# Outer combinations of x made in the round that takes them, and GpSimd's combinations in pieces of 512 columns

## The chip, the cores and the metric

The kernel runs on one core of one Trainium2 chip. The metric is the device time in microseconds of one execution; the time given is the median of several runs. A profiled execution is one run of its own: its span is the stretch that the hardware profiler covers, and its time is a little longer than the span. All data are 32-bit floats.

## The reference

Two layers, each a residual around "a convolution conditioned on a small vector, then a feed-forward". Layer 1 mixes the 128 channels with a matrix of its own per batch entry and then applies a 2048x2048 weight to the positions, with a low-rank update; layer 2 is a grouped convolution of 9 taps and a feed-forward of 16 heads on permuted rows:

```python
agg_w = einsum('bk,koi->boi', att, weight)          # layer 1: att from cond
y = einsum('boi,bih->boh', agg_w, x) + agg_b
out = einsum('bsd,od->bso', y, W) + bias + upd      # upd: low rank, from A and Bf
x = x + out
...
x = x + unpermute(down(gelu(up(permute(conv(x) + ctx)))))   # layer 2
```

x is 32 x 128 x 2048. The change touches only the product of x with the 2048x2048 weight.

## The kernel before, in words

**The product.** The kernel folds the low-rank update into the weight (16 blocks of 128x2048, in DRAM as `wb_d`) and multiplies x with it by a fast scheme of 7 products in place of 8 (Strassen's, in Winograd's form), used twice, one inside the other. The outer level gives seven **rounds**, in the order P1, P2, P6, P7, P5, P3, P4 (L48). Each round has eight **steps**, one for each group g of four batch entries; step i is round i // 8, group i % 8. The inner level gives, within a step, seven products of four 128x512 matmuls each (`multiply`, L318), which TensorE does in the order P1, P2, P6, P5, P7, P3, P4. The profile counts two matmul records for each matmul, so a step has 56.

**Left sides.** x lies in DRAM transposed, in four tiles per group: `x_load(g, tp, kh)` (L251) fetches one of 1 MB (128x2048). The outer scheme needs, per group, x00, x01, x11 as they are; s1 = x10 + x11; s2 = s1 - x00; x00 - x10 (P7); x01 - s2 (P3). Before, `x_loads` of round P1 fetches x00, x10 and x11 together, `x_combine` puts them on the list `outer`, and `x_outer` (L298) makes s1 and s2 right there on GpSimd, two operations over 2048 columns (L302, L304), and stores each in DRAM (`part_store`, on GpSimd's queue). Round P6 loads s2, round P5 loads s1, round P3 loads x01 and s2. `x_combine` (L275) makes the outer difference where its round has one (L280 for P7, L282 for P3: one operation over 2048 columns) and then the four inner combinations into a tile `s_...` (L285 to L288, 512 columns each), all on GpSimd.

**Right sides.** `outer_weights` (L365) loads up to three weight blocks for one kc of the next round; its `combine` (L385), called a step later, makes one block of them on GpSimd over 2048 columns (L387, L389; for P6 the result is stored as t2). `inner_weights` (L232) makes from the four blocks the inner combinations on GpSimd, 512 columns each: for each block t1 (L239), t2 (L240), then b22 - b12 **written over b12** (L241), then t4 (L242). Product P6 of a step takes t2, P5 takes t1, P7 the overwritten one, P4 takes t4. For round P1 the four blocks are made first (`w_make`, L162), each is stored to DRAM from GpSimd's queue (L160), and `make_first` interleaves the making with `inner_weights`; after block 2 comes the inner combination of the first group's x. For round P2 it runs in the step of group 6, later in that of group 7.

**Results.** A step of P1 copies its sums from the PSUM banks into a fresh tile `m_P1...` (first copies on ScalarE, L329; additions on VectorE, L327); a step of a later round loads old sums from DRAM (`part_load`) and adds to them. A store on SP's queue ends each step (L363). A bank taken by a product comes free for a later one only when VectorE or ScalarE has read it.

**Order.** The order on each engine is the program's: nothing is reordered. In a step i after round P1 stand: GpSimd's `x_combine` for step i + 1; SP's loads of x for step i + 2; SP's load of old sums for i + 1; in group 7 `inner_weights` for the next round; the outer-weight combinations of the step before; in groups 2 to 5 SP's loads of outer weights; the seven products. In round P1, x is loaded one step ahead, and the steps make the other twelve weight blocks (`w_make_two`, L205, additions L213) ahead of their products, from combinations of A (`a_combine`, GpSimd) and of Bf (`b_combine`, L193; for the first of them VectorE, L196 to L199, queued behind the additions that make the first four blocks). Between the products (`between`), VectorE also makes `mixed_kernel` (L407, L409: 128x128 operations into `ags`, a pair after each of four products, in groups 0 to 5 of the rounds after P1) and, in P1, sums of weight rows (L230, L951, L952).

**Slots.** All large tiles share 24 slots of 128x2048 in SBUF. A tile takes the slot that was released longest ago, and its first writer waits until the last reader of the tile before it is done, a store included.

After round P4 comes the second layer's feed-forward (L679, L690), which the change does not touch.

Of the kernel before, what the change touches and what calls it, by code (L numbers as in the profile page):

```python
# [51 lines left out]
def adaln_ffn_kernel(  # L52
# [35 lines left out]
    def scratch(name, shape=(P, L)):  # L88
# [12 lines left out]
    ag_d = [scratch(f"ag_d{i}") for i in range(B // NCH)]  # L101
    part_d = {
        (n, g): scratch(f"{n}_d{g}")
        for n in ("s1", "s2", "p1", "u1", "u2", "u3", "c00", "c01", "c10", "c11")
        for g in range(NG)
    }

# [124 lines left out]
    def inner_weights(name, ts, between=lambda kc: None):  # L232

        t1, t2, t4 = (slot(f"{name}_t{k}", (P, 4, QW)) for k in (1, 2, 4))
        tt = nc.gpsimd.tensor_tensor
        for kc, t in enumerate(ts):
            between(kc)
            b11, b12, b21, b22 = (t[:, ki, oi] for ki in range(2) for oi in range(2))
            tt(t1[:, kc], b12, b11, ALU.subtract)  # L239
            tt(t2[:, kc], b22, t1[:, kc], ALU.subtract)  # L240
            tt(b12, b22, b12, ALU.subtract)  # L241
            tt(t4[:, kc], b21, t2[:, kc], ALU.subtract)  # L242
        return {
            "P1": [t[:, 0, 0] for t in ts], "P2": [t[:, 1, 0] for t in ts],
            "P3": [t[:, 1, 1] for t in ts], "P7": [t[:, 0, 1] for t in ts],
            "P4": [t4[:, kc] for kc in range(4)], "P5": [t1[:, kc] for kc in range(4)],
            "P6": [t2[:, kc] for kc in range(4)],
        }


    def x_load(g, tp, kh):  # L251
        t = slot(f"xt_{g}{tp}{kh}", (P, 2, 2, QW))
        nc.sync.dma_start(t.rearrange("p k s c -> p (k s c)"), xT[g, tp, kh])
        return t
# [6 lines left out]
    def part_store(n, g, t, eng=nc.gpsimd):  # L261
        eng.dma_start(part_d[n, g], t.rearrange("p k s c -> p (k s c)"))

    def x_loads(r, g):
        return {
            "P1": lambda: [x_load(g, 0, 0), x_load(g, 1, 0), x_load(g, 1, 1)],
            "P2": lambda: [x_load(g, 0, 1)],
            "P6": lambda: [part_load("s2", g)],
            "P7": lambda: [x_load(g, 0, 0), x_load(g, 1, 0)],
            "P5": lambda: [part_load("s1", g)],  # L270
            "P4": lambda: [x_load(g, 1, 1)],
            "P3": lambda: [x_load(g, 0, 1), part_load("s2", g)],
        }[r]()

    def x_combine(r, g, ts):  # L275

        a = ts[0]
        tt = nc.gpsimd.tensor_tensor
        if r == "P7":
            tt(a, a, ts[1], ALU.subtract)  # L280
        if r == "P3":
            tt(a, a, ts[1], ALU.subtract)  # L282
        s = slot(f"s_{r}{g}", (P, 4, QW))
        a11, a12, a21, a22 = a[:, 0, 0], a[:, 1, 0], a[:, 0, 1], a[:, 1, 1]
        tt(s[:, 0], a21, a22, ALU.add)  # L285
        tt(s[:, 1], s[:, 0], a11, ALU.subtract)
        tt(s[:, 2], a11, a21, ALU.subtract)
        tt(s[:, 3], a12, s[:, 1], ALU.subtract)  # L288
        if r == "P1":
            outer.append((g, ts))  # L290
        return {
            "P1": a11, "P2": a12, "P3": s[:, 3], "P4": a22,
            "P5": s[:, 0], "P6": s[:, 1], "P7": s[:, 2],
        }

    outer = []

    def x_outer():  # L298
        tt = nc.gpsimd.tensor_tensor
        while outer:  # L300
            g, (a, b, c) = outer.pop(0)
            tt(b, b, c, ALU.add)  # L302
            part_store("s1", g, b)
            tt(c, b, a, ALU.subtract)  # L304
            part_store("s2", g, c)


    ADDED = {
# [56 lines left out]
    def outer_weights(r, kc):  # L365

        def get(d):
            t = slot(f"wo_{r}{kc}", (P, 2, 2, QW))
            nc.sync.dma_start(t.rearrange("p k o c -> p (k o c)"), d)
            return t  # L370

        def w(kh, oh):
            return wb_d[kh, oh, kc]

        tt = nc.gpsimd.tensor_tensor
        srcs = {
            "P6": [w(1, 1), w(0, 1), w(0, 0)],
            "P7": [w(1, 1), w(0, 1)],
            "P5": [w(0, 1), w(0, 0)],
            "P4": [w(1, 0), t2_d[kc]],  # L380
            "P3": [w(1, 1)],
        }[r]
        ts = [get(d) for d in srcs]

        def combine():  # L385
            if len(ts) > 1:
                tt(ts[0], ts[0], ts[1], ALU.subtract)  # L387
            if len(ts) > 2:
                tt(ts[0], ts[0], ts[2], ALU.add)  # L389
                nc.gpsimd.dma_start(t2_d[kc], ts[0].rearrange("p k o c -> p (k o c)"))  # L390
            return ts[0]

        return combine
# [465 lines left out]
        b_load(1, q)  # L859
    for k in blocks[4:6]:  # L860
        wt[k] = w_load(*k)
    xs[0] += [x_load(0, 1, 0), x_load(0, 1, 1)]
    nc.gpsimd.memset(wsum, 0.0)
    lhs, sa, tb = {}, {}, {}
    sa[0] = a_combine(0, nc.gpsimd.tensor_tensor)
# [23 lines left out]
    for i, (r, g) in enumerate(steps):  # L889
        ri = i // NG  # L890
        last_round = ri + 1 == len(ROUNDS)
        if i + 1 < len(steps):
            if i + 1 not in xs:
                xs[i + 1] = x_loads(*steps[i + 1])
            if not last_round:
                lhs[i + 1] = x_combine(*steps[i + 1], xs.pop(i + 1))
                x_outer()
        if i + 2 < len(steps) and ri > 0 and not last_round:
            xs[i + 2] = x_loads(*steps[i + 2])
        if i == 0:  # L900
            olds_load(0)
        if i + 1 < len(steps) and not last_round:
            olds_load(i + 1)
        if g == NG - (1 if ri else 2) and ri < len(ROUNDS) - 1:
            nxt = inner_weights(ROUNDS[ri + 1], [nxt[kc] for kc in range(4)])

        if ri == 0:
            ks = blocks[4 + 2 * g : 6 + 2 * g]
            if ks:
                two = [wt.pop(k) for k in ks]  # L910
                w_make_two(ks, two, sa[ks[0][0]], tb[ks[0][1]])
                made.extend(ks)
                if g == 1:
                    a_scale(1, 0, 4)
                    sa[1] = a_combine(1, nc.gpsimd.tensor_tensor)
                if g == 3:
                    tb[0] = b_combine(0, nc.gpsimd.tensor_tensor)
                for k, t in zip(ks, two):
                    unsummed.append((k[1], t))
                    if k[:2] == (1, 0):  # L920
                        nxt[k[2]] = t
        elif ri + 1 < len(ROUNDS):
            for k, combine in waiting.items():
                nxt[k] = combine()
            waiting = {}
            if 2 <= g < 6:
                waiting[g - 2] = outer_weights(ROUNDS[ri + 1], g - 2)

        if last_round and g == 0:
            late_loads()  # L930
        if last_round and g == 2:

            late["te"] = mix.rearrange("p (k r) c -> p k r c", k=2)
            nc.sync.dma_start(mix.rearrange("p k c -> p (k c)"), te_d)
        k0 = 3 * (g - NG)
        if last_round:
            stage(k0, stage_first)

        def between(j):
            b = (ri - 1) * (NG - 2) + g  # L940
            if ri > 0 and g < NG - 2 and b < B and j < KEXP // 2:
                mixed_kernel(b, (2 * j, 2 * j + 1))
            if ri == 0 and j == 2:
                for k in blocks[6 + 2 * g : 8 + 2 * g]:
                    wt[k] = w_load(*k)
            if ri == 0 and j in (1, 3) and unsummed:
                row_sums(*unsummed.pop())
            if ri == 0 and j == 5 and unsummed_first:
                t = unsummed_first.pop(0)
                tt = nc.vector.tensor_tensor  # L950
                tt(wsum[:, 0, 0], wsum[:, 0, 0], t[:, 0, 0], ALU.add)  # L951
                tt(wsum[:, 0], wsum[:, 0], t[:, 1], ALU.add)  # L952
            if last_round:
                if j == 3 and i + 1 < len(steps):
                    lhs[i + 1] = x_combine(*steps[i + 1], xs.pop(i + 1))
                    olds_load(i + 1)
                if j in (2, 4):
                    stage(k0 + j // 2, stage_first)
                if j % 2:
                    stage_third(k0 + j // 2)  # L960
                else:
                    stage(k0 + j // 2, stage_second)

        multiply(r, g, lhs.pop(i), rhs, olds.pop(i), between)
        next(chain, None)
        if last_round and g >= 6:
            pair(g - 6)
        if last_round and g == 7:
            rings()
            gather_two(0)  # L970
        if g == NG - 1 and ri + 1 < len(ROUNDS):
            rhs = nxt
            nxt = {}
# [84 lines left out]
```

## Time and profile before

| What | us |
|---|---|
| Time, median of 3 runs (2677.62 to 2681.15) | 2679.33 |
| The profiled execution, its own time | 2674.35 |
| Its span | 2672.6 |
| TensorE busy, 6484 matmul records | 2623.7 |
| VectorE busy | 1385.7 |
| GpSimd busy | 1142.4 |
| ScalarE busy | 535.1 |
| Start of round P1's first product | 48.6 |
| Start of round P2 / P6 / P7 / P5 / P3 | 333.9 / 526.3 / 718.5 / 913.9 / 1106.2 |
| Start of the feed-forward | 1547 |

A stretch line of the profile gives the bounds of a stretch, its length, the busy time of each engine with the number of instructions, the granted clock of TensorE (1.00 is full speed), the share of the DMA engines and the rate. A line of waits reads "engine, what waited, what ended the wait: total, times, longest". A line of the chain of waits gives start, length and what ran. A line of the timeline gives start, length, engine, line, operation, out<-in, shapes and, in brackets, the idle time before it and what ended it.

### The profile page before, as it was taken

Reading aid. Unit: us, or ns where it says so; the run is one execution under the profiler, and the core shown is the slowest. Engines: PE = TensorE matmul, PEld = TensorE weight load, DVE = VectorE, ACT = ScalarE, POOL = GpSimd, SP = SyncE. Lnnn points to the kernel's source line nnn. Section 1 sums busy time; section 2 is a strip of 40 time slices with the busy share of each in tenths; the row PEclk is TensorE's granted clock in tenths of the full one; section 3 lists DMA queues with packets and bytes.
Section 4 is the critical chain, followed back from the end, with each engine's and each line's share of the span. In section 5 each row is a group of like instructions: output and inputs, shape, how many; then the busy total and the mean of one; then the engine's idle time right before and its main releaser. Section 6 shows DMA issues by size and latency. Waiting matters only on the chain.

```text
span 2672.6 us, 19881 instructions
## 1 busy us (share of the span) xinstructions
PE 2623.7 (98%) x6484; PEld 1234.4 (46%) x6484; DVE 1385.7 (52%) x2168; ACT 535.1 (20%) x1103; POOL 1142.4 (43%) x770
## 2 busy tenths in 40 slices
PE   7899999999999999999999999999999999999998
PEld 3344444444444444444444455545455554555543
DVE  3666145233255355454256666666666666666610
ACT  0000100000000000000001144444444444444432
POOL 6655636624646521755323223434333343333222
PEclk9899999999999999999999999999999999999999
DMA  7786557535456466556575788777787777877532
GB/s 314 276 319 253 217 204 306 200 144 223 189 206 262 161 265 249 219 226 236 194 258 174 246 296 282 234 229 234 243 251 226 228 227 233 249 234 235 164 127 87
DMA packets 183607, 609.16 MB, mean 228 GB/s; under 512 B 16848, under 2 KB 88016, under 8 KB 139088
## 3 DMA queue, kind: packets, MB, share of 16 engines
q1 hardware_dynamic: 148928, 466.40, 49.5%
q0 software_dynamic: 34144, 140.53, 15.3%
q8 instruction: 52, 0.85, 0.1%
q10 hardware_dynamic: 432, 0.96, 0.1%
q14 instruction: 51, 0.42, 0.0%
HBM read 364.03 MB, written 210.24 MB: 215 GB/s over the span
## 4 chain that ended last, share of the span: by engine, by line
PE 92%; DVE 4%; POOL 2%; issue 1%; DMA 1%; SPq 0%; ACT 0%; POOLq 0%; DVEq 0%; ACTq 0%
PE bank L334 47%; PE bank L679 16%; PE bank L690 16%; PE bank L537 6%; PE bank L447 4%; PE bank L210 2%; DVE ags L409 2%; DVE u L327 0%; DVE vb L516 0%; DMA ws<-in_ffw 0%; DVE vb L519 0%; DVE va L517 0%; DMA a_sb<-in_A 0%; DVE va L518 0%; POOL wsum L874 0%
## 5 line engine op out<-in xcount | busy, mean ns | idle before, releaser
L679 PE MATMUL bank<-t,ws 128*128 128x512 f32 x1024 | 460.4, 592 | 0.2 <-DMA ws<-in_ffw 0.2
L690 PE MATMUL bank<-gl,ws 128*128 128x512 f32 x1024 | 460.2, 592 | 0.0
L334 PE MATMUL bank<-P_t,s_P 128*128 128x512 f32 x896 | 395.6, 595 | 22.3 <-ACT m_P L329 22.3
L697 POOL DMA_INDIRECT out<-t,orow x128 | 152.6, 1192 | 568.7 <-DVE t L695 496.2
L682 ACT ACTIVATE gl<-bank 128x512 f32<-128x512 f32 x512 | 306.2, 598 | 445.9 <-PE bank L679 443.5
L327 DVE TENSOR_TENSOR u<-bank,u 128x512 f32<-128x512 f32 x280 | 187.3, 687 | 389.6 <-PE bank L334 380.5
L690 PEld LDWEIGHTS bank<-gl,ws 128*128 128x128 f32 x1024 | 194.8, 190 | 232.7 <-issue 230.8
L679 PEld LDWEIGHTS bank<-t,ws 128*128 128x128 f32 x1024 | 194.7, 190 | 226.8 <-issue 219.3
L334 PE MATMUL bank<-wo_P,s_P 128*128 128x512 f32 x640 | 285.5, 596 | 5.2 <-DVE u L327 5.2
L334 PEld LDWEIGHTS bank<-P_t,s_P 128*128 128x128 f32 x896 | 171.1, 191 | 236.9 <-issue 213.0
L438 ACT ACTIVATE bank<-w,aggb 128x512 f32<-128x512 f32 x128 | 80.8, 684 | 894.2 <-DMA w<-w_d 876.0
L695 DVE TENSOR_TENSOR t<-bank,t 128x512 f32<-128x512 f32 x128 | 87.9, 686 | 318.5 <-PE bank L690 318.5
L430 POOL TENSOR_TENSOR x<-x,fb 128x1024 f32<-128x1024 f32 x64 | 156.3, 2461 | 219.6 <-DMA x<-in_x 184.6
L327 DVE TENSOR_TENSOR p<-bank,p 128x512 f32<-128x512 f32 x112 | 77.4, 691 | 246.3 <-PE bank L334 246.0
L334 PEld LDWEIGHTS bank<-wo_P,s_P 128*128 128x128 f32 x640 | 121.5, 191 | 161.2 <-issue 148.7
L409 DVE SCALAR_TENSOR_TENSOR ags<-mix,att_bc,ags 128x128 f32<-128x128 f32 x224 | 180.1, 804 | 4.5
L334 PE MATMUL bank<-wo_P,xt 128*128 128x512 f32 x384 | 169.0, 592 | 0.0
L663 POOL DMA_INDIRECT t<-hx_d,row x128 | 125.4, 980 | 54.6 <-issue 25.2
L334 PE MATMUL bank<-P_t,xt 128*128 128x512 f32 x320 | 144.0, 593 | 0.1
L285 POOL TENSOR_TENSOR s_P<-xt 128x512 f32<-128x512 f32 x40 | 51.6, 1290 | 203.6 <-DMA xt<-in_xT 181.0
L537 PE MATMUL bank<-va,tw_l 128*128 128x256 f32 x512 | 123.3, 382 | 7.2 <-DVE va L520 7.2
L537 PEld LDWEIGHTS bank<-va,tw_l 128*128 128x128 f32 x512 | 97.3, 191 | 49.8 <-issue 34.7
(155 smaller groups left out, 2869.1 us busy)
## 6 DMA issues: line engine op xcount, KB each, us to landing
xt<-in_xT SPq DMA_DIRECT2D x64, 1024.0 KB, 8.8
u<-u_d SPq DMA_DIRECT2D x40, 1024.0 KB, 10.6
wo_P<-wb_d SPq DMA_DIRECT2D x36, 1024.0 KB, 12.6
u<-c_d SPq DMA_DIRECT2D x64, 512.0 KB, 6.0
x<-in_x SPq DMA_DIRECT2D x32, 1024.0 KB, 7.8
xg<-x SPq DMA_DIRECT2D x256, 128.0 KB, 5.7
hx_d<-x1t SPq DMA_DIRECT2D x32, 1024.0 KB, 5.3
hx_d<-ht SPq DMA_DIRECT2D x32, 1024.0 KB, 7.2
```

What stands on the lines that cost most here:

```text
L327: nc.vector.tensor_tensor(to, ps, to, ALU.add)
L334: nc.tensor.matmul(ps, lhsT=lhs[k][:, bass.ts(kc, P)], rhs=rhs[k][kc], start=first and kc == 0, stop=last and kc == 3, skip_group_check=True,)
L409: nc.vector.scalar_tensor_tensor(ag, mix[:, k], att, ag, ALU.mult, ALU.add)
L430: nc.gpsimd.tensor_tensor(xt[:, f : f + 2], xt[:, f : f + 2], late["fb"][:, f : f + 2], ALU.add)
L447: nc.tensor.matmul(pm, lhsT=ag, rhs=u[:, f], start=False, stop=True, skip_group_check=True)
L537: nc.tensor.matmul(out, lhsT=w[:, 2 * i + r], rhs=rhs, start=first and r == 0, stop=last and r == 1, skip_group_check=True,)
L663: nc.gpsimd.indirect_dma_start(out=t.rearrange("p k t -> p (k t)"), out_offset=None, in_=hx_d[g].rearrange("l k t -> l (k t)"), in_offset= ...
L679: nc.tensor.matmul(pu, lhsT=w[:, m * P : (m + 1) * P], rhs=t[:, 0], start=True, stop=True)
L682: nc.scalar.activation(gl[m], pu, AF.Gelu)
L690: nc.tensor.matmul(pd, lhsT=w[:, (MC + m) * P : (MC + m + 1) * P], rhs=gl[m], start=(m == 0), stop=(m == MC - 1),)
L695: nc.vector.tensor_tensor(t[:, 1], pd, t[:, 1], ALU.add)
L697: nc.gpsimd.indirect_dma_start(out=out, out_offset=bass.IndirectOffsetOnAxis(ap=orow[:, g, h : h + 1], axis=0), in_=t[:, 1], in_offset=None,)
```

## The change

1. Round P1 loads only x00. `x_outer`, the list `outer` and the tensor s1 in DRAM are gone.
2. Round P6 loads x10, x11 and x00, makes s1 in place of x10 and s2 in place of x11, and stores s2 (which P3 still loads). Round P5 loads x10 and x11 and adds them.
3. GpSimd's operations over 2048 columns on x and on outer weights become four over 512 columns each (`pieces`).
4. In `inner_weights`, the operations that overwrite b12 stand after those of all four blocks, not within each block.

```diff
@@ inner_weights
             tt(t1[:, kc], b12, b11, ALU.subtract)
             tt(t2[:, kc], b22, t1[:, kc], ALU.subtract)
-            tt(b12, b22, b12, ALU.subtract)
             tt(t4[:, kc], b21, t2[:, kc], ALU.subtract)
+        for t in ts:
+            tt(t[:, 0, 1], t[:, 1, 1], t[:, 0, 1], ALU.subtract)
...
+    def pieces(out, a, b, op):
+        for i in range(2):
+            for j in range(2):
+                nc.gpsimd.tensor_tensor(out[:, i, j], a[:, i, j], b[:, i, j], op)
+
     def x_loads(r, g):
         return {
-            "P1": lambda: [x_load(g, 0, 0), x_load(g, 1, 0), x_load(g, 1, 1)],
+            "P1": lambda: [x_load(g, 0, 0)],
             "P2": lambda: [x_load(g, 0, 1)],
-            "P6": lambda: [part_load("s2", g)],
+            "P6": lambda: [x_load(g, 1, 0), x_load(g, 1, 1), x_load(g, 0, 0)],
             "P7": lambda: [x_load(g, 0, 0), x_load(g, 1, 0)],
-            "P5": lambda: [part_load("s1", g)],
+            "P5": lambda: [x_load(g, 1, 0), x_load(g, 1, 1)],
...
@@ x_combine
-        if r == "P7":
-            tt(a, a, ts[1], ALU.subtract)
-        if r == "P3":
-            tt(a, a, ts[1], ALU.subtract)
+        if r == "P6":
+            b, a, c = ts
+            pieces(b, b, a, ALU.add)
+            pieces(a, b, c, ALU.subtract)
+            part_store("s2", g, a)
+        if r in ("P7", "P5", "P3"):
+            pieces(a, a, ts[1], ALU.add if r == "P5" else ALU.subtract)
...
-        if r == "P1":
-            outer.append((g, ts))
...
-    def x_outer():
-        tt = nc.gpsimd.tensor_tensor
-        while outer:
-            g, (a, b, c) = outer.pop(0)
-            tt(b, b, c, ALU.add)
-            part_store("s1", g, b)
-            tt(c, b, a, ALU.subtract)
-            part_store("s2", g, c)
...
@@ outer_weights, combine
             if len(ts) > 1:
-                tt(ts[0], ts[0], ts[1], ALU.subtract)
+                pieces(ts[0], ts[0], ts[1], ALU.subtract)
             if len(ts) > 2:
-                tt(ts[0], ts[0], ts[2], ALU.add)
+                pieces(ts[0], ts[0], ts[2], ALU.add)
...
@@ the body
-    xs[0] += [x_load(0, 1, 0), x_load(0, 1, 1)]
...
                 lhs[i + 1] = x_combine(*steps[i + 1], xs.pop(i + 1))
-                x_outer()
```

More of the change, by code (lines that the diff above doesn't have):

```diff
@@ L103, in adaln_ffn_kernel @@
         (n, g): scratch(f"{n}_d{g}")
-        for n in ("s1", "s2", "p1", "u1", "u2", "u3", "c00", "c01", "c10", "c11")
+        for n in ("s2", "p1", "u1", "u2", "u3", "c00", "c01", "c10", "c11")
         for g in range(NG)
@@ L294, in x_combine @@
         }
-    outer = []
-    def x_outer():
-        tt = nc.gpsimd.tensor_tensor
-        while outer:
-            g, (a, b, c) = outer.pop(0)
-            tt(b, b, c, ALU.add)
-            part_store("s1", g, b)
-            tt(c, b, a, ALU.subtract)
-            part_store("s2", g, c)
     ADDED = {
@@ L373, in w @@
             return wb_d[kh, oh, kc]
-        tt = nc.gpsimd.tensor_tensor
         srcs = {
```

## Prediction

> **What bounds the kernel now.** I read the page first, then the stages, then what TensorE waited for in each, then the chain of waits where it waited longest. TensorE is busy for 2623.7 of 2672.6 us, so only some 49 us are open to any change. The stages are the time up to the first product of round P1, then the rounds P1, P2, P6, P7, P5, P3 (columns: PE busy, PEld, DVE, ACT, POOL, clock, DMA share, GB/s):
>
> ```profile
> 0.00:48.60 48.60, 45.27 (x105) 21.45 (x106) 24.09 (x39) 0.00 (x0) 27.38 (x29) 1.00 0.94 368
> 48.60:333.90 285.30, 262.00 (x623) 117.20 (x622) 140.57 (x164) 25.59 (x42) 173.82 (x112) 0.96 0.66 260
> 333.90:526.30 192.40, 192.40 (x450) 85.32 (x449) 75.64 (x110) 2.41 (x4) 103.83 (x65) 1.00 0.60 232
> 526.30:718.50 192.20, 192.20 (x450) 85.18 (x449) 64.29 (x104) 0.00 (x0) 85.28 (x53) 1.00 0.48 186
> 718.50:913.90 195.40, 193.46 (x449) 84.81 (x448) 86.39 (x105) 0.00 (x0) 107.17 (x61) 1.00 0.55 215
> 913.90:1106.20 192.30, 192.30 (x450) 85.28 (x449) 98.67 (x161) 0.00 (x0) 59.86 (x46) 1.00 0.61 240
> 1106.20:1301.20 195.00, 193.21 (x450) 84.90 (x449) 88.13 (x106) 0.00 (x0) 114.30 (x63) 1.00 0.54 210
> ```
>
> P2, P6 and P5 have no idle TensorE at all: 192.3 us for 8 steps, 24.03 a step. P1 holds one big hole, and P7 and P3 are each about 3 us too long. The hole, in the waits of TensorE and in the chain:
>
> ```profile
> PE bank L334 <- ACT m_P L329: 22.3, 1, 22.3
> ```
>
> ```profile
> 66.88 4.46 POOL xt L302
> 71.62 4.16 DMA s_d<-xt
> 75.94 1.28 ACT L329
> 77.87 19.26 PE bank L334 x40
> ```
>
> The first copy into the result tile m_P1 waits until the store of s1 has landed, because that tile gets the slot of the x tile holding s1; the chain passes through GpSimd's outer combination at L302. GpSimd was late besides, since the overwriting operation L241 waited for its block's store (10.2 us in all):
>
> ```profile
> 27.69 1.27 POOL L241 TENSOR_TENSOR w<-w 128x512 f32<-128x512 f32 x1 [4.11 <-DMA wb_d<-w]
> 39.60 1.27 POOL L241 TENSOR_TENSOR w<-w 128x512 f32<-128x512 f32 x1 [5.03 <-DMA wb_d<-w]
> ```
>
> The loss in P7 is a VectorE pair queued ahead of an addition that frees a bank, beside one 128x2048 operation of GpSimd; in P6, beside 128x512 ones, the same pair is short. VectorE and GpSimd in P7, then VectorE in P6:
>
> ```profile
> 728.73 5.84 DVE L409 SCALAR_TENSOR_TENSOR ags<-mix,att_bc,ags 128x128 f32<-128x128 f32 x2
> ```
>
> ```profile
> 728.57 4.50 POOL L280 TENSOR_TENSOR xt<-xt,xt 128x2048 f32<-128x2048 f32 x1 [8.46 <-DMA xt<-in_xT]
> ```
>
> ```profile
> 560.49 2.54 DVE L409 SCALAR_TENSOR_TENSOR ags<-mix,att_bc,ags 128x128 f32<-128x128 f32 x2
> ```
>
> **What the Trainium skill says.** (1) "SBUF — State Buffer", section "Who interferes with whom": a VectorE instruction with two SBUF inputs contends with a GpSimd instruction that reads SBUF, and the loser is blocked for the whole instruction. The trace agrees: such a pair takes 0.73 us alone, 2.54 beside 512 columns, 5.84 beside 2048. (2) "TensorE: Matmul & The Clock Gate", Part 1: after an idle window of about 3.4 us the clock halves, and it takes about 3.4 us of work to come back. The trace agrees: after the hole 40 matmul records took 19.09 us (77.87 to 96.96) where 40 take 17.17 elsewhere, 1.92 us more.
>
> **The change part by part.**
>
> *Round P1 without outer combinations.* Per group, two x loads, two 4.5 us operations and two stores leave. Up to the first m_P1 that is four loads fewer, so four more slots: 24 slots had to serve 26 tiles by then (warm, whose slot is used again, 4 A/B, wsum, 6 w, 6 x, sa, three t, tb, two s, m_P1), now they serve 22. m_P1 waits for no slot, and its copy can follow its product. What is late next? TensorE finishes P2 of the first step at 55.6 and wants t2 of all four blocks for P6. GpSimd ended that at 59.4; without L241's waits its work from 18.98 is 4 stores (2.4 us) and 20 operations of 1.26 (25.2), so about 46.6, and the last block, evicted at 36.6, allows 42.3. The four overwriting operations, now last, end near 52-54, and P7 wants them at about 62. Nothing is late; the hole of 22.26 goes with its 1.92 of slow clock.
>
> One new cost: b_combine (L196-199, VectorE, two SBUF inputs) ran at 36.56 to 39.1 while GpSimd stood idle at L241 (34.57 to 39.60). Now GpSimd works there. An operation of 128x128 beside 512 columns took 1.3 us instead of 0.35; b_combine's run 0.33 longer, so some 1.65 each, less 0.4 for the first: 6.2 us for four instead of 2.6. The additions L213 that free the banks stand behind it, so TensorE waits about 3.6 us more there (from 0, if they don't meet, to 5.3, if each waits out 1.26 and then runs 0.69). Start: -22.26 - 1.92 + 3.6 = **-20.6 us**. Of 1.1 us of small waits later in P1 (L213, ctxb), less contention should give some 0.5 back: **-0.5**.
>
> *Pieces of 512 columns.* 2048 columns cost GpSimd 4 x 1.264 = 5.06 instead of 4.51 us, beside other work. A blocked VectorE pair falls from 5.84 to about 2.6 us; with the addition (0.69) that is 3.3, within the 3.43 between two products, so it no longer pushes the bank back. P7 spans 718.54 to 913.96 by the stores that end its steps, 195.42 against 192.27 for P6: **-3.15**. P3: 1106.23 to 1301.24, 195.01: **-2.74**. In P5 each addition is doubled: 1.38 + 2.6 = 4.0 exceeds 3.43 by 0.55, for at most three products while GpSimd's 10 us last: 1.65 us, within the slack of 3.43 - 1.38 = 2.05. Zero.
>
> *Round P6.* Per step two loads and one store more, on SP's queue ahead of the load of the old sums and of the outer weights, the store on GpSimd's queue. GpSimd: 12 x 1.264 + store 0.87 = 16.1 us, 21.1 with an outer-weight combination, in 24.03: it fits. DMA, in the four fullest steps: 3 x, 1 old, 2 weights, 2 stores = 8 x 1.049 MB = 8.4 MB in 24.03 us = 349 GB/s; early on, the same queues moved 420 for 20 us. It fits. Latency: two x tiles issued at 718.96 were in use at 728.57, 9.6 us; a third adds 2.5 at 420 GB/s. So tiles asked for at the start of step i are ready combined at +12 to 13 + 16 = +29 us, wanted at +48: 19 us of cover. The tightest place is the turn to P6, where 16 inner operations (20.2 us) stand ahead of the second group: its combination should end near 546, wanted from 550 on (s only at 557). Slots: 7 weights, 2+2 left sides, 3 x, 2 old, 1 ags = 17, and up to 7 of the next round (with x then 2): 23 or 24 of 24, plus those not yet drained; waits, but on releases a step old. Cost taken: **0**, bounds 0 to 12 us (each of 8 steps 1.5 late). *P5*: one load in place of a load, one more load, 5.06 us of GpSimd in 24: zero. Total bytes: 7 transfers per group before and after.
>
> *Overwriting last* in later rounds waits less or equally: zero.
>
> Sum: -20.6 - 0.5 - 3.15 - 2.74 = **-27.0**. The span goes from 2672.6 to 2645.6, the profiled execution from 2674.35 to 2647.3; the median lies 4.98 above it, so **2652.3 us**.
>
> **Rivals.** (A) *P6 is starved, slower than before.* If slots run so short that a group's loads start only when GpSimd has finished the group before, load and combination add up: 13 + 16.1 = 29.1 a step, and with four weight combinations (20.2) 253 us instead of 192. Less 19 of lead, +42; with -27, **2694 us**. It decides the sign once the round loses over 27. For it: 24 slots for 24 tiles. Against: the slots handed over are a step old. (B) *Another wait takes the hole's place* (m_P1's new slot, or a store): only P7 and P3 gain, 2679.3 - 5.9 = **2673.4**. Against: four slots are freed ahead of it. (C) *Pieces don't do it*, VectorE stays pushed back: 2679.3 - 21.1 = **2658**. Against: P6's row. (D) P6 loses its bound of 12: **2664**.
>
> **How the numbers follow.** Forecast 0.66, C 0.10, D 0.08, B 0.06, A 0.10. The forecast's own range: -31.4 (no cost at b_combine, all small waits gone) gives 2648, and with the spread of the runs (1.7) 2646; upward C and D: 2668 with the same spread and b_combine's dear end. What is left out is A and B, 0.16. A measurement here tells about 0.2% (5.4 us) from no change. Faster: 0.66 + 0.10 + 0.08 and half of B = 0.87; same: the other half and an A of middling size, 0.05; slower 0.08.
>
> **What would show it.** Right: no wait of TensorE on m_P L329; b_combine near 1.6 us each and a wait on L213 of some 4 us near 40; P7 and P3 at 192.3 like P6; P6 still 192.3, GpSimd some 150-170 us busy in it, 290-350 GB/s. Wrong: TensorE waiting for s_P (L285-288) or for old sums in P6, or m_P L329 still waiting for a DMA.

## The result, and the profile after

The time is 2651.59 us (median) against 2679.11 for the kernel before, measured together: a ratio of 0.9892, 95% interval 0.9878 to 0.9905, so 1.1% faster. The forecast was 2652.3. The profiled execution of after took 2649.93 us, its span 2648.2. One of the six executions of after took 3075.58 us at a granted clock of 0.85; it counts in the median above and not in the ratio, and without it the median is 2649.93.

Stages of the kernel after (the columns are those of the same view of before), from the end of the start on: P1, P2, P6, P7, P5, P3.

```profile
53.40:314.40 261.00, 259.95 (x623) 116.67 (x622) 112.05 (x164) 24.32 (x41) 79.81 (x70) 1.00 0.39 152
314.40:506.80 192.40, 192.40 (x450) 85.32 (x449) 71.18 (x110) 2.41 (x4) 114.61 (x94) 1.00 0.67 259
506.80:699.00 192.20, 192.20 (x450) 85.19 (x449) 76.19 (x104) 0.00 (x0) 163.83 (x137) 1.00 0.74 290
699.00:891.30 192.30, 192.30 (x450) 85.28 (x449) 68.04 (x105) 0.00 (x0) 114.57 (x93) 1.00 0.59 229
891.30:1083.60 192.30, 192.30 (x450) 85.25 (x449) 98.89 (x160) 0.00 (x0) 97.53 (x79) 1.00 0.69 273
1083.60:1275.80 192.20, 192.20 (x450) 85.16 (x449) 72.05 (x105) 0.00 (x0) 121.12 (x98) 1.00 0.55 213
```

All five rounds from P2 to P3 now take 192.2 to 192.4 us, with TensorE busy all through. The work has moved: DMA in P1 falls from 260 to 152 GB/s, in P6 it rises from 186 to 290; GpSimd's busy time falls from 173.8 to 79.8 us in P1 and rises from 85.3 to 163.8 in P6. What TensorE still waited for, longest first:

```profile
PE bank L534 <- DVE va L517: 7.8, 6, 3.8
PE bank L210 <- DVE w L213: 4.7, 3, 4.0
PE bank L332 <- DVE u L325: 1.5, 1, 1.5
```

The wait of 22.3 us on ScalarE's copy into m_P1 is not among them. A new one of 4.0 us at L213 is (0.6 before). It is read from TensorE, VectorE and GpSimd at that place, in this order. First TensorE and VectorE in the kernel before:

```profile
39.92 5.39 PE L210 MATMUL bank<-tb,sa 128*128 128x512 f32 x12 [0.57 <-DVE w L213]
```

```profile
36.56 0.68 DVE L196 TENSOR_TENSOR tb<-bf_sb 128x512 f32<-128x512 f32 x1
```

Then the three in the kernel after:

```profile
43.09 7.08 PE L210 MATMUL bank<-tb,sa 128*128 128x512 f32 x12 [3.98 <-DVE w L213]
...
53.44 7.03 PE L332 MATMUL bank<-w,xt 128*128 128x512 f32 x16
```

```profile
36.32 1.01 DVE L196 TENSOR_TENSOR tb<-bf_sb 128x512 f32<-128x512 f32 x1
37.37 1.64 DVE L197 TENSOR_TENSOR tb<-bf_sb,tb 128x512 f32<-128x512 f32 x1
38.93 1.75 DVE L198 TENSOR_TENSOR tb<-bf_sb 128x512 f32<-128x512 f32 x1
40.59 1.75 DVE L199 TENSOR_TENSOR tb<-bf_sb,tb 128x512 f32<-128x512 f32 x1
```

```profile
36.74 1.71 POOL L870 TENSOR_TENSOR wsum<-wsum,w 128x512 f32<-128x512 f32 x1
38.41 1.71 POOL L239 TENSOR_TENSOR P_t<-w 128x512 f32<-128x512 f32 x1
```

VectorE's four operations of b_combine, 0.69 us each before, take 1.0 to 1.75 now, in step with GpSimd's, which take 1.71 instead of 1.27. TensorE waits 3.98 us behind them and then runs twelve records in 7.08 us that took 5.39 before: the granted clock is 0.50 from 43.9 to 47.3. So the first product of P1 starts at 53.44 instead of 48.58.

### The profile page after: what moved, and what is told of

Read it like the earlier page. It is cut to its first block, busy times and chain, and to the rows that moved or that the text cites. A ratio compares the mean times of both kernels' runs of the same rounds, so it can differ in the third digit from the quotient of the medians.

```text
span 2648.2 us, 20100 instructions
## 1 busy us (share of the span) xinstructions
PE 2620.2 (99%) x6484; PEld 1234.3 (47%) x6484; DVE 1335.3 (50%) x2168; ACT 535.2 (20%) x1103; POOL 1200.2 (45%) x950
## 4 chain that ended last, share of the span: by engine, by line
PE 95%; DVE 2%; DMA 1%; issue 1%; SPq 0%; ACT 0%; POOLq 0%; DVEq 0%; ACTq 0%
PE bank L332 49%; PE bank L676 16%; PE bank L687 16%; PE bank L534 6%; PE bank L444 4%; PE bank L210 2%; PE bank L172 1%; DMA xg<-x 1%; DVE va L514 0%; DVE vb L513 0%; DVE vb L516 0%; DMA ws<-in_ffw 0%; DVE va L515 0%; DVE va L517 0%; DMA bf_sb<-in_BfT 0%
## 5 line engine op out<-in xcount | busy, mean ns | idle before, releaser
L687 PEld LDWEIGHTS bank<-gl,ws 128*128 128x128 f32 x1024 | 194.8, 190 | 232.7 <-issue 230.8
L676 PEld LDWEIGHTS bank<-t,ws 128*128 128x128 f32 x1024 | 194.6, 190 | 228.0 <-issue 219.2
L332 PE MATMUL bank<-wo_P,xt 128*128 128x512 f32 x640 | 281.5, 592 | 0.0
L269 POOL TENSOR_TENSOR xt<-xt,xt 128x512 f32<-128x512 f32 x128 | 159.6, 1280 | 157.7 <-DMA xt<-in_xT 157.7
L332 PE MATMUL bank<-P_t,xt 128*128 128x512 f32 x448 | 201.5, 593 | 0.0
L296 POOL TENSOR_TENSOR s_P<-xt 128x512 f32<-128x512 f32 x56 | 71.8, 1283 | 272.1 <-DMA xt<-in_xT 215.8
L332 PEld LDWEIGHTS bank<-wo_P,xt 128*128 128x128 f32 x640 | 121.7, 190 | 152.1 <-issue 150.1
L406 DVE SCALAR_TENSOR_TENSOR ags<-mix,att_bc,ags 128x128 f32<-128x128 f32 x224 | 155.9, 696 | 4.5
```

Of the source, the lines that this page charges most:

```text
L269: nc.gpsimd.tensor_tensor(out[:, i, j], a[:, i, j], b[:, i, j], op)
L332: nc.tensor.matmul(ps, lhsT=lhs[k][:, bass.ts(kc, P)], rhs=rhs[k][kc], start=first and kc == 0, stop=last and kc == 3, skip_group_check=True,)
L406: nc.vector.scalar_tensor_tensor(ag, mix[:, k], att, ag, ALU.mult, ALU.add)
L676: nc.tensor.matmul(pu, lhsT=w[:, m * P : (m + 1) * P], rhs=t[:, 0], start=True, stop=True)
L687: nc.tensor.matmul(pd, lhsT=w[:, (MC + m) * P : (MC + m + 1) * P], rhs=gl[m], start=(m == 0), stop=(m == MC - 1),)
```

## The experiments

The kernels were measured in three groups, each beside runs of the kernel before, whose median there was 2677.44, 2676.14 and 2677.71 us. So groups are compared by ratio, and stages by the stores that end the steps of each profile (in P5, which has two stores a step, by the first). A profile is one execution, and its stages vary: six kernels of the table do the same work up to the end of the first step (after, after without pieces, pieces of 1024, weights whole, x of P6 a step later, 23 slots), and they end it at 77.4 to 80.1 us.

| Kernel | us | Ratio, 95% interval | End of first step | P6 | P7 | P5 | P3 |
|---|---|---|---|---|---|---|---|
| before | 2679.11 | 1 | 97.8 | 192.3 | 195.4 | 192.3 | 195.0 |
| after | 2651.59 | 0.9892 (0.9878-0.9905) | 78.3 | 192.3 | 192.3 | 192.3 | 192.3 |
| overwriting last alone | 2670.34 | 0.9968 (0.9955-0.9980) | 91.8 | 192.3 | 195.5 | 192.3 | 195.5 |
| pieces alone | 2678.41 | 1.0003 (0.9994-1.0012) | 99.0 | 192.3 | 192.3 | 192.3 | 192.3 |
| move alone | 2691.16 | 1.0043 (1.0031-1.0056) | 80.2 | 226.6 | 195.5 | 197.1 | 194.6 |
| after without pieces | 2691.81 | 1.0056 (1.0039-1.0073) | 77.4 | 219.9 | 194.8 | 196.5 | 196.0 |
| after, pieces of 1024 | 2653.93 | 0.9915 (0.9899-0.9932) | 80.1 | 193.7 | 192.3 | 192.3 | 192.3 |
| after, weights whole | 2651.54 | one run | 79.4 | 192.3 | 192.3 | 192.3 | 192.3 |
| after, x of P6 a step later | 2665.10 | one run | 78.1 | 203.0 | 192.3 | 192.3 | 192.3 |
| after, 23 slots | 2671.57 | one run | 77.9 | 192.3 | 192.3 | 192.3 | 192.3 |
| after, b_combine on GpSimd | 2644.65 | 0.9877 (0.9860-0.9893) | 74.1 | 192.3 | 192.3 | 192.3 | 192.3 |
| the same again | 2644.82 | 0.9880 (0.9864-0.9897) | 73.4 | 192.3 | 192.3 | 192.3 | 192.3 |
| the same, bias in pieces | 2640.26 | 0.9863 (0.9846-0.9879) | 72.9 | 192.3 | 192.3 | 192.3 | 192.3 |

My theory was the prediction's: the gain is the hole (a slot) and the blocked VectorE pairs of P7 and P3, and P6 is covered. The rivals: P6 starved; pieces without effect; another wait in the hole's place.

### After without pieces

```diff
     def pieces(out, a, b, op):
-        for i in range(2):
-            for j in range(2):
-                nc.gpsimd.tensor_tensor(out[:, i, j], a[:, i, j], b[:, i, j], op)
+        nc.gpsimd.tensor_tensor(out, a, b, op)
```

> After, but GpSimd's combinations of x and of outer weights again as one operation over 2048 columns each (what is made where stays). Theory (one GpSimd operation blocks a VectorE pair for its whole length): P7 and P3 are 195 us again instead of 192.3, together +5.9; P6, which now has two such operations a step, and P5, with doubled additions, lose too: up to 3.4 us a step in six steps of P6 and up to 1.7 a step in six of P5, so a total of 2657.5 to 2687, 2668 taken. Rival (the 3 us in P7 and P3 came from the loads and GpSimd being late, not from the length of an operation): P6, P7, P5, P3 all stay at 192.3, 2651.6.

Measured: 2691.81, slower than before. P7 and P3 are long again (+2.5, +3.8), P5 loses 4.2 and P6 27.6, more than the 20 I allowed; the total lies above the range given. VectorE, GpSimd and TensorE of one step of P6 in this kernel:

```profile
546.77 9.09 DVE L404 SCALAR_TENSOR_TENSOR ags<-mix,att_bc,ags 128x128 f32<-128x128 f32 x2
```

```profile
546.64 9.07 POOL L267 TENSOR_TENSOR xt<-xt,xt 128x2048 f32<-128x2048 f32 x2 [11.08 <-DMA xt<-in_xT]
```

```profile
556.61 6.28 PE L330 MATMUL bank<-wo_P,s_P 128*128 128x512 f32 x8 [3.62 <-DVE p L323]
```

Each operation of the pair waits out one whole operation of GpSimd: the pair takes 9.09 us, the two operations of GpSimd beside it 9.07. TensorE then waits 3.62 us, and after so long a pause eight records take 6.28 us instead of 3.60. This second part I had left out of the bound: in all of P6 TensorE's waits for these additions are 17.1 us, and the other 10 of the 27.6 are slow clock (TensorE is busy for 202.6 us in the round instead of 192.2). A control lies in the same run: the steps of groups 6 and 7, which have no such pair, take 24.03 us, those of groups 0 to 2 take 30.5 to 30.7, and those of groups 3 to 5 lie between (25.1 to 29.7).

### The move alone

The edit above, and in `inner_weights` the overwriting back between t2 and t4 of each block.

> After, but with whole operations over 2048 columns and the overwriting within each block: only the outer combinations are moved. Theory: m_P1 waits for no slot, TensorE waits for t2 of block 4 at about 59.5, so a hole of 3.9 us is left instead of 22.3, and b_combine is not disturbed: the start is as good as in after within 1 us (gain 18.5 to 20.3), P7 and P3 195 again, P6 and P5 as in the run with whole operations: 2668, within 2 us of that run. Rival (overwriting last is needed for the start): start 5 us or more worse than after.

Measured: 2691.16 (2682.68 to 2699.04), P6 226.6; the profile is of the slowest of these runs. Moving alone takes the hole away: TensorE has no wait on m_P1. The total is that of the run without pieces, as expected. The first step ends at 80.2, 1.9 us later than in after but hardly above the 77.4 to 80.1 us of the six kernels with the new order of overwriting, so no cost of the old order is shown, and the rival's 5 us did not come. Two parts of the expectation fell: b_combine was disturbed here too, with a wait of 3.8 us at L213, because GpSimd came out of its wait at L241 at 37.6 and met it, and the 3.9 us of waiting for t2 did not come, since the products start later (at 55.35) and t2 is ready when TensorE gets to it. So "overwriting last" is not needed for that collision: it came in both orders, when GpSimd had work there.

### Overwriting last alone

In the kernel before:

```diff
-            tt(b12, b22, b12, ALU.subtract)
             tt(t4[:, kc], b21, t2[:, kc], ALU.subtract)
+        for t in ts:
+            tt(t[:, 0, 1], t[:, 1, 1], t[:, 0, 1], ALU.subtract)
```

> Before, with nothing changed but the overwriting operations of inner_weights last. Theory (m_P1 waits for the store of s1, and GpSimd reaches s1 earlier by what it waited at L241): s1 is made some 8 us earlier, the hole of 22.3 us shrinks, but b_combine now meets GpSimd as in after; end of the first step at about 89 instead of 97: 2671. Rival (only the slots count): hole moves with nothing gained, 2679; or b_combine's delay is added in full: 2684.

Measured: 2670.34. The hole is 11.2 us instead of 22.3, and the chain still leads through the store of s1, only earlier (TensorE, then the chain):

```profile
70.94 9.94 PE L335 MATMUL bank<-P_t,s_P 128*128 128x512 f32 x16 [11.21 <-ACT m_P L330]
```

```profile
59.94 4.46 POOL xt L303
...
64.69 4.17 DMA s_d<-xt
...
69.01 1.28 ACT L330
```

The same operation (L302) ran at 66.88 in the kernel before, 59.94 here: the 7 us come out of the 10.2 us of waits at L241, the only operation that the edit moves. The step ends 5.9 us earlier, at 91.8 where about 89 was expected; the wait of 4.5 us at L213 takes some of it, and so does the clock (sixteen records take 9.94 us behind the pause, 7.03 elsewhere).

### Pieces alone

In the kernel before, every operation of GpSimd over 2048 columns as four of 512, those of `x_outer` too.

> Before, with nothing changed but the pieces of 512 columns (outer combinations still in P1, overwriting still within each block). Theory (parts act each in its own place): P7 and P3 are 192.3, -5.9; the start keeps its hole, longer by 0.6 (s1 takes 5.06 instead of 4.51): 5.3 under the kernel before, a ratio of 0.998. Rival (pieces cost GpSimd more than they give): at or above the kernel before.

Measured: no difference (0.9994 to 1.0012). P7 and P3 are 192.3, as expected, 5.9 us gained. But P1 lost 9.0, where I had allowed 0.6: 1.2 up to the end of the first step, 7.8 later. Pieces are not cheap there: beside VectorE's sums of weight rows, four of them took 8.48 us where the whole operation took 4.51 (GpSimd and VectorE here, then GpSimd in the kernel before):

```profile
118.39 8.48 POOL L268 TENSOR_TENSOR xt<-xt,xt 128x512 f32<-128x512 f32 x4 [1.09 <-DMA xt<-in_xT]
```

```profile
117.92 7.83 DVE L230 TENSOR_TENSOR wsum<-wsum,w 128x1024 f32<-128x1024 f32 x4
```

```profile
114.21 4.51 POOL L302 TENSOR_TENSOR xt<-xt,xt 128x2048 f32<-128x2048 f32 x1
```

VectorE also waited in P1 for weight blocks:

```profile
DVE w L213 <- DMA w<-in_WT: 7.7, 2, 4.4
```

The same wait was 1.7 us in the kernel before. The stores of the finished weight blocks stand on GpSimd's queue behind `x_outer`; the first pair of them in the second step is issued 34.6 us after the step's start here (133.56 against 98.96), 27.3 before (125.03 against 97.77), and the slots of those blocks come free with them. That the longer pieces and these stores are the whole of the 7.8 us is argued from these lines, not shown by a run.

### Pieces of 1024 columns; weights whole

Pieces of half a tile: two operations `out[:, i]` instead of four. And, apart, `outer_weights` with whole operations, x in pieces of 512.

> After, with pieces of 1024 columns. Theory (a VectorE pair may take 5.5 us before a bank is late: 6.86 between an addition and the use of its bank, less the addition and what stands ahead): a pair takes at most 2 x 2.45 = 4.9 us, so P7, P3 and P6 stay at 192.3; in P5, with doubled additions, 1.4 + 4.9 exceeds the 5.5 by 0.8, in up to six steps, at most 5 us: 2652 to 2657. Rival (any pair longer than the 3.4 us between two products costs): P6, P7, P3 lose 1.5 us a step in six steps, 2675 or more.

> After, with only the outer weights combined over 2048 columns at once again; x stays in pieces. Theory (what must be short is what meets VectorE's pairs in every step): the weights are combined in three or four steps of a round and hold up one pair each, P2 stays at 192.4, P6 and P7 lose up to 0.7 us in each of four steps, 0 to 5 us in all. Rival (the weights' pieces carry the gain): P6 is more than 10 us longer.

Halves: P7, P3 and also P5 are 192.3, P6 loses 1.4 us; 2653.93. A pair of P7 in this kernel:

```profile
736.55 4.75 DVE L405 SCALAR_TENSOR_TENSOR ags<-mix,att_bc,ags 128x128 f32<-128x128 f32 x2
```

So a pair may take 4.75 us, far more than the 3.4 us between two products, before a bank is late; at 5.84, in P7 of the kernel before, it was late. This fits a limit set by the distance to the next use of the bank. The 5 us allowed for P5 did not come. Weights whole, in its one run: no stage changes. In these rounds the pieces are needed for x only.

### P6's x a step later; 23 slots

```diff
-        if i + 2 < len(steps) and ri > 0 and not last_round:
+        if i + 2 < len(steps) and ri > 0 and not last_round and steps[i + 2][0] != "P6":
```

> After, with P6's three x tiles asked for one step ahead instead of two. Theory (the round is covered by some 19 us, and the turn to it by less): tiles are ready combined 29 us after they are asked for, wanted 24 us after (the part for the inner combinations 31 us after), so little is lost inside the round, but at the turn the inner weights, queued behind the first group's combination, come some 12 us late: P6 is 205 to 225 us instead of 192.3. Rival (P6 has cover to spare and doesn't need the early load): P6 stays within 3 us of 192.3.

> After, with 23 slots instead of 24. Theory (tiles taken in P6 wait for releases that are a step old): one slot less is still covered, P6, P7, P5 and P3 stay within 3 us of 192.3; at the start 22 tiles fit, so the start is as in after. Rival (P6 fits 24 slots just so): P6 is 200 us or more.

Later loads: P6 203.0, just below the range given, and all of the loss in the first step (34.7 us); the other seven are 24.03 or 24.04. TensorE waited there for the inner weights, which stand on GpSimd's queue behind the first group's combination:

```profile
PE bank L332 <- POOL P_t L240: 6.0, 3, 2.8
```

These waits are 6.0 of the 10.7 us; most of the rest is slow clock (0.50 from 518.5 to 528.7). So inside the round even one step of lead is enough, and the cover that matters is at the turn. With 23 slots the start and P1 to P3 are unchanged, so P6 is not at the edge of its slots either; the 20 us lost in this one run come in the second layer (from the end of P3 on 1394 us instead of 1372). Rival A is out on both counts.

### The first b_combine on GpSimd, and the bias in pieces

```diff
         if kc == 2:
+            tb[1] = b_combine(1, nc.gpsimd.tensor_tensor)
             lhs[0] = x_combine(*steps[0], xs.pop(0))
...
-    tb[1] = b_combine(1, nc.vector.tensor_tensor)
```

> After, with the first b_combine made by GpSimd ahead of the first group's inner combination instead of by VectorE. Theory (the wait of 4.0 us at L213 and the 1.7 us of slow clock behind it come from VectorE and GpSimd blocking each other): the wait falls to about 0.6, P1's first product starts at 48.4 instead of 53.4, all else the same: 2646.7. Rival (GpSimd's 5 us more come back as a wait for t2 or for the overwritten blocks): start of P1's P6 or P7 late by up to 5, 2651.6 or more.

> The first b_combine on GpSimd once more, beside the run with the bias in pieces on the same chip: a ratio to the kernel before of 0.988, as before; its P6 starts after 67 us less than 503.

(The last clause of the second gives no number that could be compared.) Measured twice, 2644.65 and 2644.82: 0.12 to 0.15 points below after by the ratios, whose intervals overlap, so the gain rests on the first step. The wait at L213 falls to 0.6, the clock stays up, and the first step ends at 74.1 and 73.4, 4.2 and 4.9 us earlier than in after and below all six of the 77.4 to 80.1. GpSimd's four more operations come back nowhere: product P6 of the first step follows P2 without a gap.

The last version also cuts the addition of the feed-forward bias, which GpSimd does from P4 on over 1024 columns, into pieces of 512:

```diff
-        for f in (0, 2):
-            nc.gpsimd.tensor_tensor(
-                xt[:, f : f + 2], xt[:, f : f + 2], late["fb"][:, f : f + 2], ALU.add
-            )
+        for f in range(4):
+            nc.gpsimd.tensor_tensor(xt[:, f], xt[:, f], late["fb"][:, f], ALU.add)
```

> After, with the first b_combine on GpSimd and also the addition of the feed-forward bias on GpSimd (64 operations over 1024 columns, from round P4 on) in pieces of 512. Theory (TensorE's 9 us of waits for VectorE in P4 come in part from VectorE standing behind these operations): those waits fall by 2 to 5 us, 2641 to 2644. Rival (those waits come from VectorE's own work at that place, or from the four inner combinations, already of 512 columns): same as with b_combine on GpSimd alone, within 1.5 us.

Measured: 2640.26 (2638.32 to 2643.30), against 2644.82 (2644.07 to 2646.93) on the same chip, 4.6 us or 0.17%, a little more than expected. TensorE's waits for va without and with it:

```profile
PE bank L534 <- DVE va L517: 8.2, 7, 3.7
```

```profile
PE bank L532 <- DVE va L515: 6.7, 7, 2.4
```

These fall by only 1.5 us, and without this edit they already vary more from kernel to kernel (7.8 in after, 6.3 with pieces of 1024, 9.4 with weights whole). From the end of P3 on this profile takes 1368.3 us, the two of the version without the edit 1370.3 and 1372.2. So the gain is in the times, but the expected cause is not shown; where it comes from stays open. This version is the fastest tried, 0.9863 of the kernel before.

## Why the prediction was right, point by point

**The hole (right).** -22.26 and -1.92 of slow clock came as worked out, no other wait took the place, and the two slot-related experiments show why: without the four early loads it is gone (the move alone), with the loads and an earlier s1 it is only halved (overwriting last alone). The move takes away loads, combinations and stores together, and no run separates them; that it is the slot is read from the chain, which leads through the store of s1 both times.

**b_combine (right in kind, short in size).** The term was 3.6 us; the first product starts 4.86 later. The wait itself was 3.98 instead of 0.57, so 3.4 more, close to the term; what the step left out is the clock behind it, 7.08 - 5.39 = 1.7 us, though the prediction quotes the same rule for the hole. (TensorE had come to this place 0.24 us earlier.) The start gave 19.5 (97.77 to 78.29), not 20.6; by the six kernels that start alike it would be 17.7 to 20.4.

**Small waits in P1 (wrong, 0.5).** From the first step to the end of P1 nothing changed: 19.50 ahead at its end.

**P7 and P3 (right, with too strict a limit).** Both take 192.27: -3.16 and -2.75. The limit was not the 3.43 us between two products that the prediction gives: with pieces of 1024 columns pairs of 4.75 us cost nothing in P7. It did no harm, as the pairs now stay below both limits. A pair of P7 in the kernel after:

```profile
709.23 2.54 DVE L406 SCALAR_TENSOR_TENSOR ags<-mix,att_bc,ags 128x128 f32<-128x128 f32 x2
```

**P6 and P5 at zero (right).** GpSimd was busy 163.8 us and the rate 290 GB/s, as the prediction's last paragraph named. Of three x tiles issued from 531.22 on, the first two, which are all that the first addition reads, are in use at 543.90, 12.7 us later. The prediction had 9.6 for two tiles and 12 to 13 for three, so the loads are slower than it took them to be; that it did no harm is due to the 19 us of cover. SP's queue, then GpSimd:

```profile
531.22 2.46 SPq L254 DMA_DIRECT2D xt<-in_xT  x3
```

```profile
543.90 9.93 POOL L269 TENSOR_TENSOR xt<-xt,xt 128x512 f32<-128x512 f32 x8 [6.17 <-DMA xt<-in_xT]
```

**The sum.** At the end of P3 the kernel is 25.4 us ahead, 27.0 forecast: 1.1 too much was taken for the start and 0.5 for the small waits. From there on the profile of after takes 1372.3 us, that of before 1371.3; but four more profiles with this second layer (pieces of 1024, weights whole, b_combine on GpSimd twice) take 1370.3 to 1372.9, so that 1.0 can't be told from nothing. The spans differ by 24.4, the medians by 27.5, and by 29.2 with 2649.93 for after. So the sum is 2.6 us too large by the profiles and 2.2 too small by that last figure, and that the median was met within 0.7 us is in part luck. (The terms of the lower end, -31.4, add up to -31.2; its 2648 stands.)

**What the prediction priced wrongly without harm: rival C.** "Pieces don't do it" was put at 2658, faster than before, counting only that P7 and P3 then gain nothing. Without pieces the kernel takes 2691.8, since the move puts two operations of 2048 columns into every step of P6, which was clean. It should have been the rival on the slower side. Pieces are not a third gain beside the move but the condition for it: alone the parts give -8.6 us (last, by its ratio), +0.8 (pieces) and +11.5 (move), together +3.7; the change gives -29 by its ratio.

## What to carry to other kernels

When GpSimd work is moved to a stage, look at what VectorE does there with two SBUF inputs: the length of a single GpSimd operation, not their sum, decides how late VectorE gets. Cutting 2048 columns into four cost GpSimd little in P6 (eight pieces 9.93 us, two whole operations 9.07), but up to 4 us beside VectorE's long sums in P1 (8.48 instead of 4.51): there the pieces make GpSimd the one that waits. A wait of an engine for its output tile's slot is removed by holding fewer tiles ahead of it, and a wait on a queue that is taken away lets its engine run into others that had the place to themselves. In these runs a pause of TensorE of some 4 us was paid twice, as the pause and as 1.7 to 2.8 us of slower clock behind it.

## What the runs showed of the hardware that I had not expected

- Two VectorE operations of 0.35 us in a row wait out one GpSimd operation each: the pair took 9.09 us beside 9.07 us of GpSimd, and 0.73 alone. GpSimd's next operation starts at 551.22, before VectorE's second gets its turn at 551.32.
- Beside 128x512 operations of VectorE with two SBUF inputs (0.69 us alone), GpSimd's own of 1.27 us stretch to 1.59 to 1.71; beside 128x128 ones (0.35 us) only to 1.32.
- Four pieces of GpSimd beside VectorE's 128x1024 sums took 8.48 us, where one operation over the same columns took 4.51.
- What a pause costs in clock differs from run to run. At L213 twelve records take 5.39 us; they took 7.08 behind a pause of 3.98 us (after, granted clock 0.50 for 3.4 us) and 8.23 behind one of 3.80 us (the move alone, 0.50 for 6.8 us). With x of P6 a step later, three pauses of 1.4, 2.8 and 1.8 us with two records between them brought it to 0.50 for 10.2 us.
